# Four image layers on one core: where the constants of the scans are made, and where their first pixels are loaded

## The chip, the cores and the metric

One core of a Trainium2 chip runs the whole kernel. The metric is the device time in microseconds (us); the time of a kernel is the median of several executions. Times inside an execution come from the hardware profiler. It names the engines PE (matrix products), PEld (its weight loads), DVE (vector), ACT (scalar and table functions), POOL (GpSimd) and SP (which here only issues transfers; ACT issues some, too). PSUM is the memory that PE writes to, in eight banks; SBUF is the working memory; DRAM is the memory outside the engines.

## The reference

The input is x of shape (4, 64, 128, 128) in float32: four images of 64 channels. Four layers follow each other. The first is a gate in the spectrum with attention; the second mixes Fourier modes and routes to experts; both are left out here.

The third layer goes through a Hartley transform: it takes 20 x 20 modes of each channel, mixes the channels mode by mode, goes back to pixels, smooths along all four axes and keeps a band of columns:

```python
def _L2_conv_ref(x, w1):
    x_ht = dht_2d(x)
    out_ht = jnp.zeros((B, Cout, H, W), dtype=x.dtype)
    out_ht = out_ht.at[:, :, :M1, :M2].set(compl_mul2d(x_ht[:, :, :M1, :M2], w1))
    y = dht_2d(out_ht) / (H * W)
    y = gaussian_smoothing_4d(y)
    return y * mask
```

The fourth layer runs two selective scans (state of 16 per channel). The spectral one ("spe") takes each pixel as a sequence of 8 groups of 8 channels, the spatial one ("spa") all pixels of all images as one sequence. Each does:

```python
def mamba_fwd(x, in_w, conv_w, conv_b, xproj_w, dt_w, dt_b, A_log, D, out_w):
    xi, z = jnp.split(x @ in_w.T, 2, axis=-1)
    xc = jax.nn.silu(causal_conv4(xi) + conv_b)
    dt, Bm, Cm = jnp.split(xc @ xproj_w.T, [dt_rank, dt_rank + D_STATE], axis=-1)
    dt = jax.nn.softplus(dt @ dt_w.T + dt_b)
    # h = exp(dt * A) * h + dt * Bm * xc ;  y = h . Cm + D * xc
    return (y * jax.nn.silu(z)) @ out_w.T
```

Both results are normalized in groups, put through silu, weighted by a softmax of two numbers (`att_w`) and added to the layer's input.

## The kernel before

**The stages.** `layers_0_to_2` runs the first three layers. For each of the four images it does the gate, the attention, the mixing, the experts and `hartley`, which leaves 20 x 20 modes of the image in the tile `xht` (400 x 2 x 4 numbers on each of 128 partitions). Then `hartley_back` mixes and returns to pixels for all images together. `layer3` follows with the scans.

**`hartley_back`, the way back.** First come four groups of mode products: the weights `mw` arrive in halves, one from SP's queue and one from ACT's (L1192), behind the table `pack_g`; PE multiplies them by columns of `xht`. Then comes a loop over the image rows, four at a time. `over_p(h4)` makes a pair of banks (`ps_s`, 32 small products), which DVE and ACT copy to `dt` in turn (`move`). `over_q(h4)` makes for each half of the images (`bp`) four products into a bank (`ps_pt` or `ps_m`, of which there are two each). ACT copies its columns to `st`, with a margin of four columns for the scan that runs along rows (L1237); DVE copies them to `sk`, without the margin (L1238, L1239). After every eight rows, SP stores `st` into `x2s` in DRAM (L1242), and ACT's queue stores `sk` into `x2k` (L1243). `st` and `sk` exist three times. The loop calls `over_p` one step ahead of `over_q`.

**`layer3`, the scans.** It opens new pools, loads the table `pack_d` and calls `scan_constants`, which copies parts of the table to tiles of their own (`c_gm16w`, `c_gme`, `c_sel`, `c_spe_w0` and so on), makes two products of small weights on PE (into a bank of `ps_m`), takes exponentials on ACT, and scales the identity by the softmax of `att_w` (`by_0`, `by_1`, `by_x`). Then it allots the states `h`, the inputs `dB` (eight tiles each) and two tiles `A10` and `A11` for pixels of the spectral scan, clears parts of these on POOL, and calls `scans`.

The pixels of the spectral scan come in groups of four units. `spe_load(m, g)` loads one eighth of group `m` into `A1[m % 2]` by two transfers on SP of eight partitions each (L1373, L1374), so that a group takes 16 transfers; it reads `x2k`. Of a unit, `do_x` makes two sums of products and ACT makes `xc` and `zs` of them (L1400, L1401); `do_dt` makes `dt` in nine steps, in one of which the identity sums four tiles in a bank; `do_put` writes `dt` and `dtx` to DRAM and `do_copy` brings them back spread over partitions; then `do_exp`, `do_dB`, `do_scan` and `do_hc` work on eight parts, and `do_sums` and `do_y` close the unit.

**What sets the order.** Inside `scans` the order of PE, DVE, ACT and POOL is written out by hand: every step has a due time, and the steps are issued in the order of these times. SP's transfers are not part of that. Outside of it a scheduler orders the instructions of each engine by when it reckons that they can run. It also puts in the waits: for data, for a tile or bank that is used again, and for memory in which a tile of a closed pool lay. A queue executes in order, so an instruction that waits holds up those behind it.

Of the kernel before, what the change touches and what calls it, by code (L numbers as in the profile page):

```python
# [19 lines left out]
NM = 20  # L20
# [13 lines left out]
CPX = 64  # L34
ORDER = (0, 2, 4, 6, 1, 3, 5, 7)
# [276 lines left out]
class Net:  # L312
# [67 lines left out]
    def layers_0_to_2(self, x2s, x2k):  # L380
        tc, nc = self.tc, self.nc
        with ExitStack() as ctx:
            const = ctx.enter_context(tc.tile_pool(name="const", bufs=1))
            self.k = self.unpack(const, "a")
            self.eps = const.tile([128, 1], F32, name="eps")
            nc.vector.memset(self.eps, 1e-5)
            self.nmz = [const.tile([128, 4, 128], F32, name=f"nmz{i}") for i in range(2)]
            for t in self.nmz:
                nc.gpsimd.memset(t, 0.0)
            self.xht = const.tile([128, NM * NM, 2, NB], F32, name="xht")  # L390
            with tc.tile_pool(name="big", bufs=4) as big, tc.tile_pool(name="srw", bufs=1) as srw:
                self.big = big
                self.sr1 = srw.tile([128, 32, C], F32, name="sr1")
                nc.scalar.dma_start(self.sr1, self.d["sr1"])
                self.gate_constants(const)
                for b in range(NB):
                    with self.banks(f"a{b}", s=2, pt=2, m=2):
                        xf = self.spectral_gate(b)
                        kT, va, hold = self.keys_values(b, xf)
                    with self.banks(f"b{b}", sp=6, o=1, m=1):  # L400
                        xc = self.attention(b, xf, kT, va)
                    hold.close()
                    with self.banks(f"c{b}", s=2, pt=2, m=2):
                        self.fourier_mixing(b, xc)
                        self.experts(b, xc)
                        self.hartley(b, xc)
            with self.banks("d", s=2, pt=2, m=2):
                self.hartley_back(x2s, x2k)
# [770 lines left out]
    def hartley_back(self, x2s, x2k):  # L1179

        tc, nc = self.tc, self.nc
        with tc.tile_pool(name="hb", bufs=1) as hp:
# [26 lines left out]
            with tc.tile_pool(name="hs", bufs=3) as sp:  # L1209
                rows, dts = {}, {}  # L1210

# [34 lines left out]
                for h4 in range(0, N, 4):  # L1246
                    if h4 + 4 < N:
                        over_p(h4 + 4)
                    over_q(h4)

    def layer3(self, x2s, x2k, y1, ye):
        tc, nc = self.tc, self.nc
        self.x2s, self.x2k, self.y1, self.ye = x2s, x2k, y1, ye
        with ExitStack() as ctx:
            pool = lambda name, bufs: ctx.enter_context(tc.tile_pool(name=name, bufs=bufs))
            const = pool("c3", 1)
            self.psum = ctx.enter_context(tc.tile_pool(name="psum3", bufs=1, space=PSUM))
# [4 lines left out]
            with tc.tile_pool(name="d3", bufs=1) as dp:  # L1264
                self.scan_constants(const, self.unpack(dp, "d"))
# [4 lines left out]

            self.big2 = [const.tile([128, 10 * 4 * CPX + 96], F32, name=f"A1{i}") for i in range(2)]
            self.A1 = [t[:, : 10 * 4 * CPX].rearrange("p (t x) -> p t x", t=10) for t in self.big2]
            for A in self.A1:
                nc.gpsimd.memset(A[0:64, 0:3, :], 0.0)
                nc.gpsimd.memset(A[64:128, 0:2, :], 0.0)
# [3 lines left out]
            self.dBs = [const.tile([128, 2, 512], F32, name=f"dB{q}") for q in range(8)]  # L1279
# [13 lines left out]
    def scan_constants(self, pool, k):  # L1293
        nc = self.nc
        self.c3 = c3 = {}

        def keep(name, shape):
            c3[name] = pool.tile(list(shape), F32, name="c_" + name)
# [317 lines left out]
    def scans(self, us):  # L1616
# [7 lines left out]
        for ci, u in enumerate(us):  # L1624
# [4 lines left out]
            else:  # L1629
# [4 lines left out]
                for g in range(8 if i == 0 else 0):  # L1634

                    do(-48.0 + 3 * g if m > 1 else -48.0, self.spe_load, m, g)
# [133 lines left out]
    def run(self):  # L1770
        with self.tc.tile_pool(name="dram", bufs=1, space=DRAM) as dp:
# [4 lines left out]
            self.layers_0_to_2(x2s, x2k)  # L1776
            self.layer3(x2s, x2k, y1, ye)
# [21 lines left out]
```

## Time and profile before

| what | value |
|---|---|
| median of 3 runs | 7353.47 us (7347.41 to 7354.81) |
| the profiled execution | 7342.41 us |
| its span, first to last instruction | 7340.7 us |
| mean granted clock of PE | 0.953 |
| busy PE, DVE, ACT, POOL | 90%, 74%, 65%, 49% of the span |
| way back, loop over rows, about | 3440 to 3564.5 us |
| first product of the scans | 3581.65 us |

Times in views are counted from the span's start. The shares of busy time are averages over stages with different limits: POOL does almost nothing in the first half and is busy all the time in the second. A row of the chain of waits has a start, a length and the engine or transfer on which the end of the span depended there. A row of the waits has who waited, for whom, the sum in us, how often, and the longest.

### The profile page before, as it was taken

The numbers are of one execution on the slowest core, as the hardware profiler recorded it, in microseconds if no ns is written. First come the engines' busy times: TensorE is split into PE (matmuls) and PEld (weight loads), VectorE is DVE, ScalarE is ACT, GpSimd is POOL, SyncE is SP. The second block draws the span as 40 slices with busy tenths as digits, with TensorE's granted clock in tenths as the row PEclk, the third lists the DMA queues.
The fourth block names the chain that finished last, engine by engine and source line by source line (L and its number), as shares of the span: only waits on it lengthen the run. The fifth ranks groups of instructions, "written<-read, shape, count | busy, mean of one in ns | idle before, by whom it ended". The sixth has DMA issues, their size and how long they took to land.

```text
span 7340.7 us, 106844 instructions
## 1 busy us (share of the span) xinstructions
PE 6632.5 (90%) x39058; PEld 2873.7 (39%) x39058; DVE 5408.6 (74%) x7737; ACT 4771.6 (65%) x7768; POOL 3607.2 (49%) x1908
## 2 busy tenths in 40 slices
PE   8998999989999899988899999999899888888897
PEld 6335553347335553346422223222322332332333
DVE  3665546563565546663599999999999899899896
ACT  2564636553564536652588888888788787887885
POOL 1000000000000000000399999999999899899896
PEclk9998989989999989987899999999999999999998
DMA  3000010002000110002455555555454464564554
GB/s 90 1 1 1 28 47 1 1 1 74 1 1 1 28 47 1 1 1 106 133 145 150 149 147 150 149 149 148 133 149 146 129 183 142 143 172 137 156 162 119
DMA packets 364110, 647.03 MB, mean 88 GB/s; under 512 B 46784, under 2 KB 219584, under 8 KB 362048
## 3 DMA queue, kind: packets, MB, share of 16 engines
q1 hardware_dynamic: 357680, 609.91, 30.0%
q10 hardware_dynamic: 5904, 30.28, 1.2%
q8 instruction: 308, 5.05, 0.3%
q14 instruction: 218, 1.79, 0.1%
HBM read 517.80 MB, written 122.22 MB: 87 GB/s over the span
## 4 chain that ended last, share of the span: by engine, by line
PE 48%; DVE 19%; issue 10%; POOL 10%; ACT 8%; DMA 4%; SPq 1%; POOLq 0%; DVEq 0%; ACTq 0%
PE ps_sp L330 14%; DVE h L1493 9%; PE ps_s L330 8%; PE ps_m L330 7%; POOL hc L1520 6%; PE ps_o L330 6%; PE ps_pt L330 4%; DVE dB L1488 3%; POOL dB L1488 2%; PE ps_dx L330 2%; PE ps_y L330 2%; DMA s_dx<-ddx 2%; ACT dA L1472 2%; DVE big L1061 2%; PE ps_m L811 1%
## 5 line engine op out<-in xcount | busy, mean ns | idle before, releaser
L1520 POOL TENSOR_TENSOR hc<-h,C 128x966 f32<-128x966 f32 (+3 forms) x1128 | 2437.4, 2240 | 118.7 <-DVE h L1493 93.2
L1493 DVE TENSOR_TENSOR_SCAN h<-dA,h,dB 128x483 f32<-128x483 f32 (+1 forms) x1200 | 1348.4, 1166 | 54.5 <-ACT dA L1472 54.5
L755 DVE TENSOR_REDUCE nmz<-ps_sp 128x1 f32<-128x320 f32 x2048 | 895.8, 485 | 622.5 <-PE ps_sp L330 613.2
L771 ACT ACTIVATE big<-ps_sp 128x512 f32<-128x512 f32 (+1 forms) x1536 | 830.6, 592 | 720.3 <-PE ps_sp L330 719.0
L1493 DVE TENSOR_TENSOR_SCAN h<-dA,dB 128x512 f32<-128x512 f32 (+2 forms) x1072 | 1222.0, 1190 | 4.0 <-ACT dA L1472 3.9
L930 POOL TENSOR_TENSOR aw<-pack_a 128x128 f32<-128x128 f32 x8 | 3.5, 456 | 2189.8 <-PE ps_m L330 2189.8
L1488 POOL TENSOR_TENSOR dB<-s_dx,B 128x1024 f32<-128x1024 f32 (+5 forms) x450 | 993.7, 2210 | 15.4 <-DMA s_dx<-ddx 6.7
L330 PE MATMUL ps_sp<-uT,kT 32*128 32x512 f32 x3072 | 924.2, 649 | 1.4 <-ACT big L771 0.8
L330 PE MATMUL ps_dx<-dtx,c_sel 128*128 128x483 f32 (+3 forms) x1420 | 754.5, 613 | 188.0 <-DVE dB L1488 186.5
L1488 DVE TENSOR_TENSOR dB<-ps_dx,B 128x1024 f32<-128x1024 f32 (+5 forms) x750 | 810.9, 1083 | 147.4 <-PE ps_dx L330 146.5
L1472 ACT ACTIVATE dA<-s_dt,c_spa_a 128x483 f32<-128x483 f32 (+3 forms) x1232 | 760.8, 640 | 179.0 <-DVE h L1493 176.9
L330 PE MATMUL ps_sp<-kT,qT 32*128 32x320 f32 x4096 | 817.3, 499 | 3.9 <-ACT qT L736 3.3
L1472 ACT ACTIVATE dA<-s_dt,c_spe_a 128x448 f32<-128x448 f32 x1040 | 635.7, 632 | 155.0 <-DVE h L1493 154.2
L330 PE MATMUL ps_y<-hc,c_sum 128*32 128x483 f32 (+3 forms) x4512 | 680.1, 560 | 60.9 <-POOL hc L1520 54.3
L330 PEld LDWEIGHTS ps_dx<-dtx,c_sel 128*128 128x128 f32 x1420 | 225.8, 190 | 661.9 <-DVE dB L1488 225.4
L330 PEld LDWEIGHTS ps_sp<-uT,kT 32*128 32x128 f32 x3072 | 278.8, 185 | 438.3 <-issue 243.0
L330 PE MATMUL ps_o<-big,va 128*32 128x512 f32 (+1 forms) x3072 | 415.6, 613 | 0.0
L330 PE MATMUL ps_s<-pack_a,big 128*64 128x128 f32 (+4 forms) x2832 | 371.0, 307 | 45.6 <-DMA big<-in_x 19.6
L330 PEld LDWEIGHTS ps_sp<-kT,qT 32*128 32x128 f32 x4096 | 358.2, 190 | 57.2 <-issue 36.6
L330 PEld LDWEIGHTS ps_s<-pack_a,big 128*128 128x128 f32 (+2 forms) x2832 | 329.1, 180 | 67.5 <-issue 25.7
L330 PEld LDWEIGHTS ps_y<-hc,c_sum 128*32 128x32 f32 x4512 | 124.9, 109 | 509.4 <-issue 306.8
L454 POOL MEMSET big<- 64x128 f32 x4 | 0.8, 200 | 627.5 <-PE ps_s L330 420.0
(391 smaller groups left out, 10376.4 us busy)
## 6 DMA issues: line engine op xcount, KB each, us to landing
s_dt<-ddt SPq DMA_DIRECT2D x520, 256.0 KB
s_dt<-ddt SPq DMA_DIRECT2D x544, 241.5 KB
s_dx<-ddx SPq DMA_DIRECT2D x195, 256.0 KB
s_dx<-ddx SPq DMA_DIRECT2D x204, 241.5 KB
ddt<-dt SPq DMA_DIRECT2D x65, 256.0 KB
ddx<-dtx SPq DMA_DIRECT2D x65, 256.0 KB
A<-x2s SPq DMA_DIRECT2D x136, 121.2 KB
ddt<-dt SPq DMA_DIRECT2D x68, 241.5 KB
```

The source lines that it names most:

```text
L330: self.nc.tensor.matmul(out, lhsT, rhs, start=start, stop=stop)
L454: nc.gpsimd.memset(mag[64:128, 32, :], 0.0)
L755: nc.vector.tensor_reduce(self.nmz[n % 2][:, j, at : at + 1], p[:, :KEYS], AX.X, ALU.max, negate=True)
L771: nc.scalar.activation(slot(m, 2 * wu + q)[rows], p[rows], AF.Exp)
L811: nc.tensor.transpose(p[:, 128 * j : 128 * j + 128], o[:, 128 * j : 128 * j + 128], k("ident"))
L930: nc.gpsimd.tensor_tensor(aw[i], k(f"aw{i + 1}"), k("sg"), ALU.mult)
L1061: nc.vector.scalar_tensor_tensor(acc(i), y, gate[:, p : p + 1], acc(i), ALU.mult, ALU.add)
L1472: self.nc.scalar.activation(t(u["dA", q][sg][:, u["lo"] : u["n"]]), t(u["dt", q]), AF.Exp, scale=a)
L1488: eng.tensor_tensor(v(dB[:, :, x:y]), v(d), v(u["BC"][0][:, :, x:y]), ALU.mult)
L1493: self.nc.vector.tensor_tensor_scan(h[:, lo:n], u["dA", q][sg][:, lo:n], self.dBs[q][:, sg, lo:n], init, ALU.mult, ALU.add)
L1520: self.nc.gpsimd.tensor_tensor(v(hc), v(self.hs[q][:, :, at]), v(u["BC"][1][:, :, at]), ALU.mult)
```

## The change

`layer3` now opens its pool of constants first and calls `hartley_back` inside it. `hartley_back` loads `pack_d` at the start of its loop over rows, calls `scan_constants` behind the rows of `h4 == 8`, and calls `spe_load(0, g)` for all eight `g` behind those of `h4 == 80`; `scans` leaves the first group's loads out. The two lines in the loop are placed in the program's order; the scheduler may still move what they issue.

To have the memory for that at the same time, three kinds of tiles get new places. `xht` and the convolution weights `sr1` of the first layer move to a pool (`held`) that lives to the end. `A10`, the identity and the three scaled identities lie in the old `xht`, which is free after the mode products; `dB0` and `dB1` lie in the old `sr1`. The clearing of `A10` and `A11` moves into `scan_constants`.

```diff
-    def layers_0_to_2(self, x2s, x2k):
+    def layers_0_to_2(self):
...
-            self.xht = const.tile([128, NM * NM, 2, NB], F32, name="xht")
-            with tc.tile_pool(name="big", bufs=4) as big, tc.tile_pool(name="srw", bufs=1) as srw:
+            self.sr1 = self.held.tile([128, 32, C], F32, name="sr1")
+            with tc.tile_pool(name="big", bufs=4) as big:
                 self.big = big
-                self.sr1 = srw.tile([128, 32, C], F32, name="sr1")
...
-            with self.banks("d", s=2, pt=2, m=2):
-                self.hartley_back(x2s, x2k)
...
-    def hartley_back(self, x2s, x2k):
+    def hartley_back(self, x2s, x2k, const):
...
-            with tc.tile_pool(name="hs", bufs=3) as sp:
+            with tc.tile_pool(name="hs", bufs=3) as sp, tc.tile_pool(name="d3", bufs=1) as dp:
                 rows, dts = {}, {}
+                kd = self.unpack(dp, "d")
...
                     over_q(h4)
+                    if h4 == 8:
+                        self.scan_constants(const, kd)
+                    if h4 == 80:
+                        for g in range(2 * NB):
+                            self.spe_load(0, g)
...
             const = pool("c3", 1)
+            with self.banks("d", s=2, pt=2, m=2):
+                self.hartley_back(x2s, x2k, const)
...
-            with tc.tile_pool(name="d3", bufs=1) as dp:
-                self.scan_constants(const, self.unpack(dp, "d"))
...
-            self.big2 = [const.tile([128, 10 * 4 * CPX + 96], F32, name=f"A1{i}") for i in range(2)]
-            self.A1 = [t[:, : 10 * 4 * CPX].rearrange("p (t x) -> p t x", t=10) for t in self.big2]
-            for A in self.A1:
-                nc.gpsimd.memset(A[0:64, 0:3, :], 0.0)
-                nc.gpsimd.memset(A[64:128, 0:2, :], 0.0)
...
-            self.dBs = [const.tile([128, 2, 512], F32, name=f"dB{q}") for q in range(8)]
+            spare = self.held.tile([128, 32, C], F32, name="sr1").rearrange("p (i s a) c -> p i s (a c)", i=2, s=2)
+            self.dBs = [const.tile([128, 2, 512], F32, name=f"dB{q}") if q > 1 else spare[:, q] for q in range(8)]
...
     def scan_constants(self, pool, k):
         nc = self.nc
         self.c3 = c3 = {}
+        self.old_xht = self.held.tile([128, NM * NM, 2, NB], F32, name="xht").rearrange("p m s b -> p (m s b)")
+        self.big2 = [self.old_xht[:, :A1_SIZE], pool.tile([128, A1_SIZE], F32, name="A11")]
+        self.A1 = [t[:, : 10 * 4 * CPX].rearrange("p (t x) -> p t x", t=10) for t in self.big2]
+        for A in self.A1:
+            nc.gpsimd.memset(A[0:64, 0:3, :], 0.0)
+            nc.gpsimd.memset(A[64:128, 0:2, :], 0.0)
+        rest = [self.old_xht[:, A1_SIZE + 128 * i : A1_SIZE + 128 * i + 128] for i in range(4)]
...
         def keep(name, shape):
-            c3[name] = pool.tile(list(shape), F32, name="c_" + name)
+            if name in ("id", "by_0", "by_1", "by_x"):
+                c3[name] = rest.pop()
+            else:
+                c3[name] = pool.tile(list(shape), F32, name="c_" + name)
             return c3[name]
...
-                    do(-48.0 + 3 * g if m > 1 else -48.0, self.spe_load, m, g)
+                    if m:
+                        do(-48.0 + 3 * g if m > 1 else -48.0, self.spe_load, m, g)
...
-            self.layers_0_to_2(x2s, x2k)
-            self.layer3(x2s, x2k, y1, ye)
+            with self.tc.tile_pool(name="keep", bufs=1) as self.held:
+                self.xht = self.held.tile([128, NM * NM, 2, NB], F32, name="xht")
+                self.layers_0_to_2()
+                self.layer3(x2s, x2k, y1, ye)
```

More of the change, by code (lines that the diff above doesn't have):

```diff
@@ L34 @@
 CPX = 64
+A1_SIZE = 10 * 4 * CPX + 96
 ORDER = (0, 2, 4, 6, 1, 3, 5, 7)
```

## The prediction

> **What bounds the kernel now.** I first read the busy time by stage, with stages cut where the work changes: the way back of the Fourier layer (3440 to 3564.5 us), the gap behind it, the ramp of the scans, and the scans. The columns are length, busy time (instructions) of PE, PEld, DVE, ACT and POOL, granted clock, DMA share, GB/s.
>
> ```profile
> core 0: us, PE busy (x) PEld busy (x) DVE busy (x) ACT busy (x) POOL busy (x), PEclk, DMA share, GB/s
> 3440.00:3564.50 124.50, 123.53 (x1524) 89.98 (x1515) 51.14 (x144) 40.95 (x80) 0.00 (x0) 0.99 0.41 154
> 3564.50:3581.60 17.10, 0.68 (x4) 0.52 (x4) 10.20 (x51) 1.81 (x4) 2.75 (x4) 0.62 0.57 120
> 3581.60:3621.00 39.40, 28.48 (x48) 10.60 (x48) 3.64 (x4) 22.73 (x30) 7.84 (x5) 0.73 0.42 99
> 3621.00:7340.00 3719.00, 3282.52 (x12028) 1127.67 (x12026) 3451.70 (x3582) 2984.69 (x4729) 3519.33 (x1797) 0.97 0.53 148
> ```
>
> The way back is PE's: 123.5 of 124.5 us, with DVE at 41% and ACT at 33%. The scans are POOL's and DVE's (95% and 93%), and the change gives them nothing to save. Between the two lie 17.1 us in which PE does 0.68 us. That is all that a move of this kind can win, and some. The waits say who is waited for, and the chain of waits says in which order:
>
> ```profile
> PE ps_m L330 <- DMA A<-x2k: 16.4, 1, 16.4
> ```
>
> ```profile
> 3564.28 0.21 DVE sk L1239
> 3564.51 2.81 DMA x2k<-sk
> 3567.64 0.33 SPq L1373
> ...
> 3570.41 5.66 DMA A<-x2k
> 3576.09 5.50 DMA A<-x2k
> 3581.59 0.06 issue
> 3581.65 3.77 PE ps_m L330 x4
> 3585.47 1.28 ACT L1400
> 3586.76 1.17 ACT xc L1400
> ```
>
> The last store of x2k must land (3567.6) because the tiles of the scans lie where its source lay. Then SP issues 16 loads of the first pixels, some 0.7 us apart, and the first product of the scans waits for the sixteenth. The constants are not in this chain. The timeline shows them beside it, from 3567.62 to 3576.29:
>
> ```profile
> 3567.60 1.28 ACT L1315 ACT_TABLE_LOAD   x1 [3.65 <-DMA x2k<-sk]
> ...
> 3567.76 1.05 DVE L1302 COPY c_gme<-pack_d 128x512 f32<-128x512 f32 x1
> ...
> 3571.65 0.41 DVE L1310 COPY c_spa_bc<-pack_d 128x512 f32<-128x512 f32 x1
> ...
> 3576.01 0.28 DVE L1332 TENSOR_SCALAR c_by_x<-pack_d,c_att_m 128x128 f32<-128x128 f32 x1
> ```
>
> **Part 1, the gap.** In the built order of the changed kernel, the 16 loads of the first pixels stand on SP among the stores of x2s, the last of them ahead of the store of rows 80 to 87; the 16 loads of the second pixels, into memory that is now free as early, are spread in the same way, and three of them remain behind the last store. So nothing of the first load is left in the gap. What is late next? PE needs its banks: the last copy out of them ends at 3564.49, so PE starts at 3564.6 instead of 3581.65. It is now at full clock, and its four passes take 1.88 us (as the next unit's, at 3603.5) instead of 3.77, so they end at 3566.5. That is not yet the gain: ACT's first result still goes to memory that the last stores of x2s and x2k are read from, and its table load holds that wait in the built order. They landed at 3567.6; I add 0.2 us for the loads that run beside them. Table load 1.28, so xc starts at 3567.8 + 1.3 = 3569.1, against 3586.76: **17.7 us earlier**. From xc on the chain is ACT's eight steps and PE's sums, with the same instructions in the same order, none of them waiting for what was moved. The puts and copies of dt and dtx move along. The six passes at 3593.6 ran at half clock; whether they do so again depends on where idle time falls: 2 us either way.
>
> **Part 2, the constants inside the way back.** 45 instructions on DVE, 3 on ACT and 2 PE products (four passes, 0.68 us) now stand among the rows 4 to 16 of a loop that PE fills. DVE has the room on average (2.3 us idle of each 3.85), but the order has them in blocks. By the rows of before, DVE ends the first bank of rows 4 at 3450.27; then the first 21 copies follow at one go, then the second bank of rows 4, then ten more, then the two banks of rows 8. PE is released twice by these copies, since both products borrow a bank of the two that the loop's own results need: the first product (nominal 3453.99) needs the second bank of rows 4, the second product that of rows 8.
> The price of the block is the question. As traced, its 21 copies and products took from 3567.62 to 3571.98, 4.36 us, but with POOL's four memsets beside them: c_gme took 1.05 us and c_spa_bc, of the same shape, 0.41. The Trainium skill (SBUF — State Buffer, "Who interferes with whom") says that VectorE in its two-port modes and GpSimd take turns on one pair of ports, each for a whole instruction. By it the moved block, with POOL's memsets done long before, takes what its undisturbed rows give: 2.8 us (each step at its start-to-start time, 0.13 for 128x128, 0.35 for 128x512, 0.07 for a column).
> - At 2.8 us: the second bank of rows 4 is free at 3453.5, no stall at the first product. The ten others (1.6 us, with the wait for that product) and the two banks of rows 8 end at 3456.2; the second product would be due at 3454.7: stall 1.5 us. With the 0.7 us of the products PE is **2.2 us late**, and, PE being full, stays so.
> - At 4.36 us: stalls of 1.2 and 2.0 us, plus 0.7: 3.9 us late.
> I take 2.3 us, since nothing of POOL is near; ends 0.7 (all stalls absorbed) and 4.6. ACT's table load (1.28) and three exponentials there fit into its 2.5 us idle stretches, and its store of x2k waits for a DVE copy that is late by 2.8 us, which the block itself covers.
>
> **Part 3, the loads on SP and the DMA engines.** The period of eight rows is 7.69 us. SP gains two loads in most of them (six in a row once, 4.2 us): 0.7 us apart by the rows of before, and here and there a wait of 3.35 us for a store of x2k to land (issued 3564.2, landed 3567.55), beside two stores (0.65 us). That is up to 5.4 of 7.69 us; the stores that stand behind them have three buffers. The DMA engines are at 0.41 of this stage, and all 32 loads held 0.57 of them for some 22 us, 12.5 of the 73 us that are free. Cost 0; if the cover went, see the second rival.
>
> **Part 4, what the new memory layout moves.** Loads of mw and pack_g start the mode products:
>
> ```profile
> q1 hardware_dynamic: 338, 4.05, 59.6%
> q10 hardware_dynamic: 332, 2.30, 32.6%
> ```
>
> These are packets, MB and share of SP's and ACT's queue from 3355 to 3372 us. PE waits 14.05 us for the first tile of mw, of which SP's half stands behind pack_g (2.69 + 0.98 MB). In the changed order ACT's four loads, the first of which started at 3355.33, come after its copy to xht, at 3358.4. For 3 us SP then has the engines alone. At the traced share of ACT (2.30 of 6.35 MB) that frees 0.45 MB of about 0.42 MB a us: 1.1 us earlier. The Trainium skill (DMA: Bandwidth & Descriptors, "Queues, rings and completion order") says that an engine takes packets from its queues in turn; by equal turns the estimate would be 1.5 us. I take **1.1**, ends 0 and 2.
> The old tiles that now hold A10, the identity, by_* and dB0 and dB1 cost 0: in the built order the scans' instructions wait for the same engines as before.
>
> **Sum.** -17.7 + 2.3 - 1.1 = -16.5 us. The profiled execution took 7342.41 us (span 7340.7), so 7325.9 in its own terms. The median of the three runs is 7353.47, 11 us above it; the stages concerned run once, so I subtract the same: **7337.0 us**. The runs shown are 7.4 us apart, so 0.2% (14.7 us) is about what a measurement of this kernel can tell from no change, and the forecast is just beyond it.
>
> **Rivals.**
> - *The block costs what it was seen to cost, and the clock is less kind.* 4.6 us in part 2, no gain in part 4, and the passes behind xc slower by 2 us: -17.7 + 4.6 + 2 = -11.1, 7342.4 us. Also what a moderately late SP would leave. For it: c_gme's 1.05 us, and PE at half clock after 3 us of idle (from 3357.5 to 3360.3). Against it: POOL is idle there, and no single stall comes near 3 us.
> - *SP becomes the bound of the way back (slower than before).* If each of two loads in a period waited for a full landing of 3.4 us beside the store's 3.35 and 0.65 of issues, the period on SP would be 10.8 instead of 7.69 us. Over 16 periods that is 50 us, less 15.4 that three buffers forgive: 34 late, net +18, 7371 us. It decides from 7.69 us in a period. For it: loads here used about half of the engines and kept 0.7 us each. Against it: in the gap ten loads ran in 7 us without waiting for one another's landing.
> - *It doesn't do what it says*: excluded by the order, as far as the first load goes.
>
> **How the numbers follow.** Forecast and its better variants 0.62; the first rival, with a draw of the medians the wrong way, 0.27; SP's bound 0.08 and the unforeseen in the scans (1% of 3719 us would do) 0.03. The range goes from 7329 (all of part 1, 2 us of part 4, 0.7 of part 2, warm passes, and a few us of scatter) to 7347 (the first rival and 4 us of scatter).
>
> **What would show it.** Right: the first product of the scans starts within 1 us of the last copy of sk; xc 4.5 us behind that; PE in the way back stalls for 1 to 2 us once near rows 8 to 16; mode products start about 1 us earlier relative to the copy of xht. Wrong: PE waiting for a load of A at the start of the scans, SP's stores of x2s falling behind ACT's copies, or a stage of the scans that is not 3756 to 3760 us from the first product to the end (3759 now).

## The result, and the profile after

The changed kernel takes 7331.42 us, median of 11 runs (7325.84 to 7341.55), against 7353.47 us for the kernel before, also of 11 runs (7339.41 to 7356.52). The ratio is 0.9974, with a 95% interval from 0.9966 to 0.9982. The profiled execution took 7329.77 us (span 7327.9, mean granted clock 0.955), 12.6 us less than the profiled execution of before.

The busy time by stage of the changed kernel, with the same columns as the table of before, cut at the last copy of `sk` (3566.8) and at the first product of the scans (3567.0):

```profile
core 0: us, PE busy (x) PEld busy (x) DVE busy (x) ACT busy (x) POOL busy (x), PEclk, DMA share, GB/s
3441.00:3566.80 125.80, 124.85 (x1523) 90.59 (x1515) 57.13 (x189) 42.54 (x84) 0.00 (x0) 0.99 0.47 166
3566.80:3567.00 0.20, 0.00 (x0) 0.02 (x1) 0.02 (x2) 0.00 (x0) 0.00 (x0) 1.00 1.00 362
3567.00:3605.70 38.70, 26.68 (x48) 9.82 (x48) 5.60 (x8) 22.78 (x30) 7.80 (x5) 0.82 0.36 107
3605.70:7327.00 3721.30, 3283.45 (x12028) 1126.61 (x12026) 3451.42 (x3582) 2985.48 (x4729) 3520.90 (x1797) 0.97 0.54 148
```

The gap of 17.1 us is 0.2 us long. The 45 DVE instructions of the constants have moved from the gap into the way back (144 instructions there before, 189 now), where PE is as full as it was. The granted clock of the ramp is 0.82 instead of 0.73. PE's first four passes, behind 1.2 us of idle instead of 16.4, take 1.96 us instead of 3.75; the two of `c_spe_wdt`, a little later, now stand behind 3.5 us of idle instead of 1.5, and take 2.07 us instead of 1.16.

The chain of waits from the end of the way back to `xc` (start, length, engine or transfer):

```profile
3566.31 0.30 DVE sk L1237
3566.61 0.21 DVE sk L1238
3566.81 0.02 issue
3566.83 4.06 DMA x2k<-sk
3570.89 0.02 issue
3570.91 0.04 ACTq L1412
3570.95 0.03 issue
3570.98 1.28 ACT L1412
3572.26 0.01 issue
3572.27 1.18 ACT xc L1412
```

The loads of the first pixels are gone from it. What is left between the last `sk` and `xc` is the landing of the last stores, 4.2 us, and the table load.

The constants in the timeline of the changed kernel, between rows 4 and 16:

```profile
3451.27 0.42 DVE L1314 COPY c_gme<-pack_d 128x512 f32<-128x512 f32 x1
...
3453.60 0.41 DVE L1322 COPY c_spa_bc<-pack_d 128x512 f32<-128x512 f32 x1
...
3454.94 0.48 PE L331 MATMUL ps_m<-pack_d 4*128 4x128 f32 x2
...
3455.46 0.29 DVE L1325 COPY c_spa_wdt<-ps_m 128x128 f32<-128x128 f32 x1 [0.17 <-PE ps_m L331]
...
3455.92 0.48 PE L331 MATMUL ps_m<-pack_d 8*128 8x128 f32 x2
```

`c_gme` takes 0.42 us instead of 1.05, and the whole block of 21 goes from 3451.14 to 3453.93, 2.8 us.

Absolute times don't compare well between executions. Over the fourteen profiles of this study the `xm` copy of the last image, ahead of which all kernels run the same instructions (e9b issues one transfer more), starts between 3354.1 and 3367.3 us, and the stretch from the first `dB` on DVE to the end is 3722.5 to 3728.8 us long. So the stages are compared by their lengths. The table has them for all kernels, from the starts in the timelines ("mode" is the first product of `mw`, "dt" the first copy of `dt`, "sk" the end of the last copy of `sk`, "dB" the first `dB` on DVE):

| kernel | xm to mode | mode to dt | dt to sk | sk to xc | xc to dB | sum | ratio to before (95%) |
|---|---|---|---|---|---|---|---|
| before | 16.29 | 71.12 | 121.78 | 22.28 | 29.63 | 261.10 | |
| before_again | 16.95 | 71.28 | 121.78 | 22.85 | 29.38 | 262.24 | 0.9993 (0.9981 to 1.0004) |
| changed | 15.37 | 71.46 | 123.29 | 5.47 | 28.83 | 244.42 | 0.9974 (0.9966 to 0.9982) |
| after_again | 15.71 | 71.25 | 123.15 | 5.65 | 28.44 | 244.20 | 0.9980 (0.9971 to 0.9989) |
| e1_const_only | 15.61 | 71.46 | 123.62 | 20.18 | 28.71 | 259.58 | 0.9996 (0.9988 to 1.0004) |
| e2_loads_only | 15.94 | 71.38 | 121.78 | 18.77 | 29.81 | 257.68 | 0.9993 (0.9985 to 1.0001) |
| e3_loads_in_scans | 16.02 | 71.45 | 123.93 | 5.63 | 29.20 | 246.23 | 0.9976 (0.9966 to 0.9985) |
| e4_xc_memory | 15.20 | 71.45 | 124.24 | 3.54 | 28.45 | 242.88 | 0.9974 (0.9963 to 0.9985) |
| e5_second_loads | 15.11 | 71.46 | 125.62 | 5.50 | 29.78 | 247.47 | 0.9982 (0.9973 to 0.9990) |
| e6_pack_g_behind | 9.21 | 72.25 | 124.17 | 5.67 | 29.35 | 240.65 | 0.9967 (0.9955 to 0.9979) |
| e7_loads_twice | 15.24 | 71.46 | 122.73 | 5.76 | 28.87 | 244.06 | 0.9973 (0.9962 to 0.9985) |
| e8_pool_beside | 15.77 | 71.46 | 126.38 | 5.66 | 29.29 | 248.56 | 0.9976 (0.9966 to 0.9986) |
| e9b_const_in_gap | 16.17 | 71.45 | 122.52 | 9.32 | 29.79 | 249.25 | 0.9981 (0.9972 to 0.9990) |
| e11_table_early | 9.13 | 72.25 | 123.58 | 2.20 | 28.95 | 236.11 | 0.9965 (0.9953 to 0.9978) |

### The profile page after: what moved, and what is told of

Same layout as the page of the kernel before. It is cut to its first block, busy times and chain, and to the rows that moved or that the text cites. A ratio compares the mean times of both kernels' runs of the same rounds, so it can differ in the third digit from the quotient of the medians.

```text
span 7327.9 us, 106846 instructions
## 1 busy us (share of the span) xinstructions
PE 6630.8 (90%) x39058; PEld 2869.5 (39%) x39058; DVE 5405.7 (74%) x7737; ACT 4772.8 (65%) x7768; POOL 3608.7 (49%) x1908
## 4 chain that ended last, share of the span: by engine, by line
PE 49%; DVE 18%; issue 9%; POOL 9%; ACT 9%; DMA 4%; SPq 1%; POOLq 0%; DVEq 0%; ACTq 0%
PE ps_sp L331 14%; PE ps_m L331 9%; DVE h L1505 9%; PE ps_s L331 7%; PE ps_o L331 6%; POOL hc L1532 6%; PE ps_pt L331 4%; DVE dB L1500 3%; PE ps_y L331 3%; PE ps_dx L331 3%; DVE big L1059 2%; ACT dA L1484 2%; DMA s_dx<-ddx 2%; DMA big<-in_sr 1%; PE ps_m L809 1%
## 5 line engine op out<-in xcount | busy, mean ns | idle before, releaser
L1505 DVE TENSOR_TENSOR_SCAN h<-dA,h,dB 128x483 f32<-128x483 f32 (+2 forms) x900 | 1025.2, 1167 | 52.9 <-ACT dA L1484 52.9
L1505 DVE TENSOR_TENSOR_SCAN h<-dA,dB 128x512 f32<-128x512 f32 (+2 forms) x804 | 929.7, 1188 | 4.0 <-ACT dA L1484 4.0
L1500 POOL TENSOR_TENSOR dB<-s_dx,B 128x952 f32<-128x952 f32 (+6 forms) x300 | 672.6, 2244 | 14.6 <-DMA s_dx<-ddx 7.9
L1500 DVE TENSOR_TENSOR dB<-ps_dx,B 128x952 f32<-128x952 f32 (+4 forms) x600 | 646.0, 1079 | 14.5 <-PE ps_dx L331 13.7
L1505 DVE TENSOR_TENSOR_SCAN h<-dA,h,sr 128x483 f32<-128x483 f32 (+2 forms) x300 | 342.6, 1162 | 0.0
L1500 POOL TENSOR_TENSOR sr<-s_dx,B 128x952 f32<-128x952 f32 (+2 forms) x150 | 336.6, 2246 | 0.3
```

What stands on the lines that cost most here:

```text
L1500: eng.tensor_tensor(v(dB[:, :, x:y]), v(d), v(u["BC"][0][:, :, x:y]), ALU.mult)
L1505: self.nc.vector.tensor_tensor_scan(h[:, lo:n], u["dA", q][sg][:, lo:n], self.dBs[q][:, sg, lo:n], init, ALU.mult, ALU.add)
```

## The experiments

**How far one profile can be trusted: both kernels a second time.**

> The kernel before once more, for a second profile of it. Theory (the stretch from the xm copy to the first dB is steady, and the last stores of before land 3.1 us after the last sk copy): 261.1 us and 3.1 us within 0.5 us, so that the 16.7 us between the two kernels in this stretch and the 1.1 us of later landing are the change's. Rival (the landing scatters by 1 us between executions): the stores land 4 us or more after the last sk copy, and the stretch is 262 us or more, so that the changed kernel's later landing is no cost of the change.

Before again: the stores land 3.12 us after the last `sk` copy in both profiles (read at the start of the table load that waits for them), and the sum is 262.24 instead of 261.10, 1.1 us longer, which lies in the start of the mode products (0.7) and in the loads of the gap (0.6). So the landing supports the theory, and the stretch varies a little more than the theory allowed. The medians of this one program on one chip are 7344.80 and 7348.19 us.

> The changed kernel once more, as the measure for the scatter between executions. Theory (the stretch from the first dB to the end scatters by 2 us either way between executions, and the stages before the xm copy by 6 us or more): the distances from xm to the last sk copy and from there to xc come out within 1 us of the first profile of the changed kernel (210.1 and 5.5 us), and the time within 3 us of 7331.4. Rival (the 12.8 us between the two first profiles and the 22.1 us between the medians are both real and the sum missed something): the median lies 20 us or more under before again, and the stretch from xm to the first dB is shorter by more than 15 us.

The changed kernel again: 210.1 us from `xm` to the last `sk` and 5.65 to `xc`, as the theory said; the median is 7335.56 us, 4.1 above the first, a little outside of the 3 us. In the mean of two profiles each, the stretch is 261.67 us before and 244.31 after: the change gains 17.4 us there. The two ratios come to 19 and 15 us of 7350. The rival, that the 22 us between the first two medians are all the change's, falls.

**e1: constants early, loads in the gap.** On the changed kernel:

```diff
-                    if h4 == 80:
+                    if h4 == N - 4:
+                        nc.vector.tensor_copy(self.A1[0][:, 9, 0:1], rows[1][1][:, 7, 0:1])
                         for g in range(2 * NB):
                             self.spe_load(0, g)
```

> The constants stay in the way back, as in the changed kernel; the 16 loads of the first pixels are put back behind the last row group (a copy of one column of the last sk into A10 makes them wait for it). Theory (the gap was the loads, not the constants): the first product starts about 17 us after the last sk copy and xc about 22 us after it, as before the change (17.2 and 22.3), so the time is that of the kernel before, +1.4 for the constants in the way back and -0.9 for the earlier mw loads: within 2 us of before, 16 to 18 us over the changed kernel. Rival (the constants made in the gap were a share of it, the loads hid only a part): xc comes 4 us or more sooner than 22 us after the last sk copy, and the time lies that much under the kernel before.

The ratio is 0.9996: nothing is left of the gain. The chain of waits of e1 runs through the loads as that of before does:

```profile
3565.87 3.99 DMA x2k<-sk
3569.86 0.02 issue
3569.88 5.01 DMA xht<-x2k
3574.88 0.02 issue
3574.90 5.44 DMA xht<-x2k
3580.34 0.56 issue
3580.90 3.76 PE ps_m L331 x4
```

`xc` starts 20.2 us after the last `sk`, 2.4 us sooner than in the two profiles of before (22.3 and 22.9). The first seven loads start from 3565.93 on, before the stores have landed, since their memory is not that of `st` and `sk` any more. The rival asked for 4 us or more. The sum of the stretch is 2.1 us under the mean of before, and the time can't be told from it. Moving the constants alone is worth no more than that.

**e2: loads early, constants and `pack_d` behind the way back.**

```diff
-            with tc.tile_pool(name="hs", bufs=3) as sp, tc.tile_pool(name="d3", bufs=1) as dp:
+            with tc.tile_pool(name="hs", bufs=3) as sp:
...
-                    if h4 == 8:
-                        self.scan_constants(const, kd)
...
+            with tc.tile_pool(name="d3", bufs=1) as dp:
+                self.scan_constants(const, self.unpack(dp, "d"))
             self.const, self.small = const, pool("st", 2)
```

> The loads of the first pixels stay at h4 == 80; the load of pack_d and the constants go behind the way back, as before the change. Theory: pack_d is 2.42 MB, some 7 us at 350 GB/s behind its issue and the stores beside it, and the VectorE block of 2.8 us stands behind it, so that the first product starts 11 to 13 us after the last sk copy instead of 0.2, with the clock at half; the way back is 1.4 us shorter without the constants; in all 6 to 12 us over the changed kernel, and 5 to 12 us under before. Rival (the constants are hidden behind the stores' landing, which xc waits for anyway): xc starts no more than 6 us after the last sk copy, and the time is that of the changed kernel or 1.4 us less.

The ratio is 0.9993, and the sum of the stretch 4.0 us under the mean of before, against the 5 to 12 expected. But this is not what moving the loads alone is worth, and in one point the text above is wrong: before the change `pack_d` was issued at 3438.9, ahead of the way back, and only its use stood in the gap; here its load is in the gap too. What the loads alone are worth is read from e9b. The chain of waits of e2:

```profile
3565.20 10.05 DMA pack_d<-in_pack_d
3575.25 0.14 issue
3575.38 1.19 PE ps_m L331 x4
3576.57 2.36 issue
3578.93 3.77 PE ps_m L331 x4
```

`pack_d` needs 10 us beside the last stores, not 7, and 3.7 us of products and copies follow until `c_spe_w` is there. With the first product 13.65 us behind the last `sk`, the sum is 13.4 us above the changed kernel's, against 6 to 12 expected. The way back, without constants in it, takes 121.78 us to the hundredth as before; so the constants' cost there is 1.4 to 1.5 us (123.29 and 123.15). That is known to some 0.7 us: the other variants that make the same constants there have 122.7 to 124.2 (leaving out e5 and e8, which hold the loop up in other ways), and e9b, without them, has 122.5.

**e9b: only the constants in the gap.** `pack_d` lies at the other end of the memory, lands early, and the constants have memory that no store holds (two of their copies already run ahead of the last `sk`):

```diff
+            d3 = tc.tile_pool(name="d3", bufs=1, side="right")
+            self.d3 = d3.__enter__()
             with self.banks("d", s=2, pt=2, m=2):
                 self.hartley_back(x2s, x2k, const)
...
+            self.scan_constants(pool("c4", 1), self.kd)
+            d3.__exit__(None, None, None)
```

> The loads stay at h4 == 80 and pack_d lands early (in memory at the far end, issued ahead of pack_g); only the constants themselves are made behind the way back, in memory that shares nothing with st and sk, so that they need not wait for the stores. Theory (each of the two chains that the change took out of the gap fills most of it by itself, and e2's 13.7 us were pack_d's landing, 10 us, and 3.7 us of block): here the block alone stands between, so that the first product starts about 3 to 5 us after the last sk copy, xc 6 to 10 us after it instead of 5.5, and the time is 1 us less to 4 us more than the changed kernel's. Rival (the constants themselves, not their load, make e2 slow): the first product again starts 10 us or more after the last sk copy, 8 us or more over the changed kernel.

The first product starts 3.10 us after the last `sk` and `xc` 9.3 us after it, both in the theory's range. The sum is 4.9 us above the changed kernel's mean, just over the 4 us expected; the two medians (7333.48 here) are too near for the time to show it. Against before, the sum is 12.4 us shorter, and the ratio, 0.9981, is clear of 1: with the constants still in the gap, the early loads keep most of the gain. That is in the new layout; in the old one the constants waited for the last stores, too, and how much the loads alone would keep there was not run. What holds `xc` in e9b's timeline is not the product:

```profile
3580.15 3.75 PE L331 MATMUL ps_m<-xht,c_spe_w 128*128 128x512 f32 x4 [2.27 <-DVE c_spe_w L1325]
...
3584.66 0.28 DVE L1349 TENSOR_SCALAR xht<-pack_d,c_att_m 128x128 f32<-128x128 f32 x1
3585.08 1.28 ACT L1417 ACT_TABLE_LOAD   x1 [2.69 <-DVE xht L1349]
3586.37 1.18 ACT L1417 ACTIVATE xc<-ps_m,c_spe_cb 128x512 f32<-128x512 f32 x1
```

PE is at half clock again after its idle stretches (0.50 granted, 3.75 us for four passes), and the table load comes behind the last of the constants. So two chains stood side by side in the gap, if each is asked for alone: the loads (`xc` at 20.2 us, e1) and the block of constants (9.3, e9b). Taking the first away uncovers the second. The third, the landing of `pack_d` with the block behind it (18.8), was put there by e2 and stands in neither kernel.

**e3: the place in the program.**

```diff
-                    if h4 == 80:
-                        for g in range(2 * NB):
-                            self.spe_load(0, g)
...
-                    if m:
-                        do(-48.0 + 3 * g if m > 1 else -48.0, self.spe_load, m, g)
+                    do(-48.0 + 3 * g if m > 1 else -48.0, self.spe_load, m, g)
```

> Of the changed kernel only the place of the first pixels' loads in the program is undone: they stand in the scans again, the memory that they fill (the old xht) stays as the change made it. Theory (the memory lets the loads go early, the place in the program does not matter, since the queue is filled in order of readiness): the loads are issued among the stores as in the changed kernel, the first product starts within 0.5 us of the last sk copy, and the time is the changed kernel's within 2 us. Rival (the place decides): the loads stand behind the last stores, xc comes 22 us after the last sk copy, 16 us over the changed kernel.

The first product starts 0.21 us after the last `sk`, and the time is the changed kernel's (0.9976). It is the memory that lets the loads go early; where they stand in the program changes nothing.

**e7: the loads twice.**

```diff
                         for g in range(2 * NB):
                             self.spe_load(0, g)
+                            self.spe_load(0, g)
```

> The changed kernel with each of the 16 first loads issued twice (the same bytes to the same place), which adds 16 issues of about 0.55 us to the SP queue of the way back. Theory (SP has room in each row group of 7.69 us): the last sk copy comes at the same distance from the first row group within 1 us, and the time is the changed kernel's within 2 us. Rival (SP is the bound of the way back once the loads stand in it): 16 more issues lengthen the way back by up to 9 us, and the changed kernel itself paid about as much for its own 16.

122.73 us from the first `dt` to the last `sk`, not longer than the 123.15 and 123.29 of the changed kernel, and the same time (0.9973). SP has room for twice the loads; the second rival of the prediction falls. What gave way are the loads of the second pixels: most of them now start behind the last `sk`, the last one 7.8 us after it, and the stage times show no cost of that.

**e5: the second pixels' loads ahead of the last stores.**

```diff
+                    if h4 == 88:
+                        for g in range(2 * NB):
+                            self.spe_load(1, g)
...
-                    if m:
-                        do(-48.0 + 3 * g if m > 1 else -48.0, self.spe_load, m, g)
+                    if m > 1:
+                        do(-48.0 + 3 * g, self.spe_load, m, g)
```

> The changed kernel with the loads of the second pixels placed at h4 == 88, so that none of them stands in the SP queue behind or between the last stores. Theory (three loads issued with the last stores delay their landing): the table load of silu starts 3.1 us after the last sk copy, as the stores landed before the change, instead of 4.2; the time falls by 1 us. Rival (the landing of the last stores is as late without them): 4.2 us again, no change.

4.21 us again, without a single load behind the last stores, so the gain did not come. The bytes moved, in 40 slices of the six us from 3562.5 in the kernel before, of the seven us from 3564.8 in the changed kernel, and of the seven us from 3564.35 in e5:

```profile
GB/s 28 28 0 0 0 0 0 0 0 206 397 383 339 412 328 361 430 416 348 380 397 353 412 324 364 430 402 347 278 14 0 0 0 0 0 0 0 0 0 0
```

```profile
GB/s 24 24 24 0 0 0 0 0 303 379 366 416 318 380 416 392 331 404 404 303 287 220 325 419 308 274 202 154 165 193 182 111 53 29 18 0 0 0 0 0
```

```profile
GB/s 415 380 357 155 24 36 48 94 315 379 328 379 340 381 380 382 385 404 402 402 400 380 406 382 109 25 24 24 24 24 0 0 0 0 0 0 0 0 0 0
```

The stores of before end all together. In the changed kernel the last us, loads included, runs at about half of the full rate; in e5 there is a tail of 0.9 us at 24 GB/s, about one sixteenth, as if one of the 16 engines were behind. The landing signals in the traces say the same. A store has sixteen of them, a load of eight partitions eight. Those of the last store of `sk`, in us after the last copy:

| kernel | moved beside the last stores | signals of the last store |
|---|---|---|
| before, before_again | nothing | 16 from 2.65 to 2.84 |
| changed, after_again | three loads of pixels | 8 from 2.82 to 2.98, 8 from 3.55 to 4.26 |
| e2 | `pack_d` and three loads | 16 from 5.98 to 7.00 |
| e5 | one packet of instructions | 15 from 2.60 to 2.80, one at 3.83 |

All other variants have loads there, and look like the changed kernel: eight signals from 2.66 to 2.99, eight from 3.31 to 4.28. So the loads do hold up half of the landing, and the theory's mechanism holds; the rival, that the stores are as late without them, does not. What e5 gained on fifteen signals it lost on one: in each of its four last stores one signal comes 1.0 us behind the others. The packet of instructions took 0.8% of 16 engines' seven us, 0.9 us of one engine (from the view of transfers in that stretch):

```profile
q8 instruction: 1, 0.02, 0.8%
```

That it is what the late signal waited for is inferred from the two lengths, since the trace doesn't name the engine of a signal.

e5 also costs something: its way back is 2.4 us longer than in the mean of the changed kernel's two profiles. The rows of the waits in it, of SP and of PE:

```profile
SPq L1388 <- DMA x2k<-sk: 14.2, 6, 6.2
```

```profile
PE ps_pt L331 <- ACT st L1236: 2.1, 1, 2.1
```

Loads put close behind the stores that they read wait for these on SP, up to 6.2 us, with the stores of `x2s` queued behind them; then `st` is late, and so is PE. This is the mechanism of the second rival, set off by placing the loads badly. Such a wait alone does not make the cost: e7 has some of up to 6.0 us, and PE waits 0.2 us there.

**e8: POOL at work beside the constants.**

```diff
+        nc.gpsimd.tensor_copy(self.big2[1][:, :64], dt[:, :64])
+        for _ in range(3):
+            nc.gpsimd.memset(self.big2[1], 0.0)
         for key in ("gm16w", "gme", "goh", ...
```

> The changed kernel with three clears of the whole of A11 (128 x 2656) on GpSimd beside the constants, started by a copy of 64 columns of the last dt. Theory (VectorE and GpSimd share a port, so that copies that took 1.05 us beside GpSimd's clears in the gap took 0.42 us alone): the copies that stand beside the clears take 1 us instead of 0.42 (512 columns) and the block of 21 takes 4 us or more instead of 2.8. Rival (the copies of before were longer for another reason, the DMAs or the memory they lay in): 0.42 and 2.8 us again.

POOL starts at 3453.17, when the block of 21 is already done in 2.8 us; the clears meet the copies that follow (timeline of e8):

```profile
3453.17 7.31 POOL L1315 MEMSET A<- 128x2656 f32 x3
...
3453.66 2.00 DVE L1325 COPY c_spe_z<-pack_d 128x128 f32<-128x128 f32 x1
...
3455.61 2.62 DVE L1325 COPY c_spe_bc<-pack_d 128x512 f32<-128x512 f32 x1
```

`c_spe_z` took 0.22 us in the changed kernel and 2.00 here, `c_spe_bc` 0.42 and 2.62. A clear takes 2.44 us, and a copy waits out the clear that it meets. The way back grows by 3.2 us, to 126.38. So the theory holds for the mechanism, and what it says of before, that its copies were long because of POOL's four short clears, fits. Transfers are not the reason: in e9b `c_gme` ran beside the last stores without clears and took 0.42 us.

**e4: memory of their own for `xc` and `zs`.**

```diff
+            self.xz = pool("xz", 3)
             with self.banks("d", s=2, pt=2, m=2):
                 self.hartley_back(x2s, x2k, const)
...
-        u["xc"], u["zs"] = self.tile2("xc", u, 3), self.tile2("zs", u, 3)
+        u["xc"], u["zs"] = (self.xz.tile([128, 512], F32, name=key)[:, u["lo"] : n] for key in ("xc", "zs"))
```

> The changed kernel with memory of their own for xc and zs, in a pool opened before the way back, so that they share nothing with st, sk and dt. Theory (in the changed kernel xc, started 5.5 us after the last sk copy, waits for the last stores to land, because its tile lies where st and sk were): the table load for silu no longer waits for a DMA and stands beside the first products, xc starts about 2.5 us after the last sk copy, when the products end, and the time falls by about 3 us (2 to 3.4). Rival (it is the loads or something else that holds xc, or what follows xc waits for the stores all the same): xc or its followers start as in the changed kernel, and the time stays within 1 us.

The table load no longer waits for a transfer, and `xc` starts 3.54 us after the last `sk`, 1.9 to 2.1 us earlier (timeline of e4):

```profile
3576.27 1.28 ACT L1413 ACT_TABLE_LOAD   x1 [2.77 <-PE ps_m L331]
3577.56 1.17 ACT L1413 ACTIVATE xc<-ps_m,c_spe_cb 128x512 f32<-128x512 f32 x1
```

It is 1 us short of the theory, as the table load now holds `xc`'s wait for the products instead of standing beside them. The time (0.9974) can't tell 2 us.

**e6: `pack_g` behind the first weights.**

```diff
+                    if t == 0:
+                        kg = self.unpack(hp, "g", self.xht[:, NM * NM - 1, 1, NB - 1 :])
...
+        if behind is not None:
+            self.nc.vector.tensor_copy(t[:, :1], behind)
         self.nc.sync.dma_start(t, self.d[name])
```

> The changed kernel with the load of pack_g (2.69 MB) issued behind the first two halves of mw (a copy of one column of xht into it makes it wait), so that the first mode's weights have the DMA engines first. Theory (the mode products' start is set by bytes ahead of the first mw tile in the DMA engines, which is why the earlier mw loads gained 0.9 us): the products start 5 to 7 us sooner after the xm copy than the 15.4 us of the changed kernel, and the time falls by 4 to 7 us. Rival (the stage is bound by all its bytes, so that the later mw tiles or gbc are late instead): the products start sooner, but the last of them end as before, and the time stays within 1 us.

The timeline of e6:

```profile
3368.96 0.33 SPq L1189 DMA_DIRECT2D mw<-in_mw  x1
...
3370.01 0.33 SPq L346 DMA_DIRECT2D pack_g<-in_pack_g  x1
...
3375.86 12.93 PE L331 MATMUL ps_s<-xht,mw 128*64 128x8 f32 x120 [6.97 <-DMA mw<-in_mw]
```

The mode products start 9.2 us after `xm` instead of 15.4 to 15.7, and the stage behind them is 0.9 us longer: 5.4 us gained, and 0.9967. So the start of the stage is a matter of the bytes ahead of the first tile.

**e11: the three gains together, the table load first.** On e4 and e6 together:

```diff
+                    if h4 == N - 4:
+                        warm = const.tile([128, 1], F32, name="warm")
+                        nc.scalar.activation(warm, rows[1][0][:, 7, :1], AF.Silu)
```

> Three edits on the changed kernel: memory of their own for xc and zs (as in e4), the load of pack_g behind the first mw halves (as in e6), and a silu of one column of the last st into a tile that nothing reads, so that ScalarE loads its table right behind the last st copy, beside the first products. Theory (the gains stand in a row on one chain): 5.4 us from the earlier mode products, 1.9 us from xc that waits for no store, 1.3 us from the table load beside the products, so xc starts 2.2 us after the last sk copy, and the time is 8 to 9 us under the changed kernel's, some 7323 us. Rival (what is gained before the scans is given back in them, or the table load pushes the last x2k stores back and these hold the next step): the stage times fall as said, but the time stays within 3 us of the changed kernel's.

`xc` starts 2.20 us after the last `sk`, as said, and the median is 7323.21 us (0.9965): the best of all, 8 us under the first median of the changed kernel and 12 under the second. Its interval overlaps that of the changed kernel, so the stage times carry the claim: 236.11 against 244.31 us. One part of the rival is there too. In the chain of waits of e11 the wait for the last stores has moved one step on, to the table load of `sp_hi`:

```profile
3572.01 0.21 DVE sk L1241
3572.22 0.02 issue
3572.24 4.13 DMA x2k<-sk
3576.37 0.02 issue
3576.39 0.04 ACTq L1432
3576.43 0.13 issue
3576.56 1.28 ACT L1421
3577.84 0.01 issue
3577.86 0.69 ACT sp_hi L1432
```

`sp_hi` starts 5.65 us after the last `sk`, 3.2 us earlier than in the changed kernel (3575.68 against 3566.80, 8.9 us) and about as much as `xc` (3.3). The 4.13 us of landing are now the longest piece there.

## Why the prediction was right, point by point

The forecast was 7337.0 us, a gain of 16.5; the median came out at 7331.4, a gain of 22.1. By stages, as the mean of two profiles each, the gain is 17.4.

- *What bounds the kernel.* Right: the gap was all that could be won, way back and scans gave nothing, and the loads were the longer chain in it. What the prediction did not ask is what each half of the change is worth. Of the 17.4 us, the early loads alone, in the new layout, keep 12.4 (e9b) and the early constants alone 2.1 (e1); the last 5 us need both. Both were moved in one change, so its sum did not need that point.
- *Part 1, -17.7.* From the last `sk` to `xc` -17.0: 22.57 before in the mean, 5.56 now. The step that was mis-sized is "I add 0.2 us for the loads that run beside them": the stores land 4.2 and 4.35 us after the last `sk`, where they landed after 3.12 us in both profiles of before, so the term is 1.1 to 1.2 us. The landing signals show the loads to be the cause (e5); e4 shows that this landing does hold `xc`. The clock, "2 us either way", came out at -0.9 from `xc` to `dB`, which is not clear of the scatter: the variants with `xc` as early have 28.4 to 29.8 there.
- *Part 2, +2.3.* +1.4 (123.22 against 121.78), within the ends 0.7 and 4.6. The choice between the two prices of the block was right: 2.8 us, as the rule of the Trainium skill (SBUF — State Buffer, "Who interferes with whom") had it, not the 4.36 us of the traced block. e8 shows the rule at work. The mis-sized term is the stall, put at 1.5 us beside 0.7 for the products: the products took 0.96 (the two rows above), so that 0.5 us are left for stalls. The one stall of 1 to 2 us that was to show it is not there: the waits of PE have no row in those rows of the loop.
- *Part 3, 0.* Right, and with room to spare (e7). The second rival needed 10.8 us in a period; only e5, with loads right behind the stores that they read, shows its mechanism, at 2.4 us. One reading against that rival was wrong: the loads in the gap did wait for one another's landing. In the chain that the prediction shows, the load of 3576.09 starts as that of 3570.41, the eighth before it, lands; the first eight start 0.35 us apart, and only the later ones 0.7. It did no harm, as e7 shows.
- *Part 4, -1.1.* -1.1 (16.62 before, 15.54 now, in the mean of two). The wait itself is one row of the waits of the changed kernel:

```profile
PE ps_s L331 <- DMA mw<-in_mw: 13.1, 1, 13.1
```

It was 14.05 us before. Equal turns of the queues would have given 1.5. The runs don't decide between the two: the two profiles of before differ by 0.7 us in this stage, so that the agreement to a tenth is luck. That the stage hangs on the bytes ahead of its first tile, e6 shows.
- *Sum.* -17.0 - 0.9 + 1.4 - 1.1 is -17.5 before rounding, and the 0.2 us that the stage from mode to `dt` is longer make it -17.4; the prediction's -16.5 is within 1 us, in part by luck: its terms missed by 0.7 us (part 1), 0.9 (the clock) and 0.9 (part 2), not all the same way. The other 5 us of the first pair of medians are not the change's as far as shown: medians of the same program differ by 3 us (before_again) and 4 us (after_again), and the first profiles alone would give 12.8 us of span.

Most of the prediction's signs were there, too: the first product 0.2 us after the last `sk`, and `xc` 5.3 us behind that instead of 4.5. The mode products start 0.9 us sooner by the first pair of profiles. From the first product to the end it is 3760.9 us in the first profile, 0.9 above the 3756 to 3760 foretold, and 3759.6 in the second; before again has 3760.0.

## What to carry to other kernels

A gap between two stages can be several chains side by side. The profile names the one that ends last, and taking that one away gains only what it is longer than the next (here 12.4 of 17.4 us), so list what else starts at the gap's beginning and ask of each when it would end by itself. An experiment that takes one half of a change back can put something new into the gap, as e2 did with `pack_d`: look at what it moved before believing its time. What keeps work from starting early can be the memory of a closed pool and not the place in the program: find the first instruction that waits for a transfer only because of where its tile lies. And for a gain of 0.2%, compare lengths of stages between two marks in the profile, not absolute times or single spans.

## What the runs showed of the hardware that was not expected

- The last stores (two of 276 KB and two of 260 KB) landed 3.12 us after the last copy in both profiles of before, and 4.0 to 4.5 us after it where loads of eight partitions were issued beside them. Only half of the last store's sixteen landing signals were late (e5); beside `pack_d` all were, by 3.3 us or more (e2).
- One signal of sixteen, 1.0 us late, is enough to hold a store as long as three loads do (e5: 4.21 us). The packet of instructions that fits it is of 16 KB, and took 0.95 us.
- A VectorE copy that meets a GpSimd clear of 2.44 us takes up to 2.62 us instead of 0.42 (e8).
- SP had eight loads in flight in the gap of before: from the ninth on, each started when the load eight before it had landed (the first 2.6 us after its issue, the ninth 5.7).
- The first four passes of the scans took 3.77 us behind 11.1 and 2.4 us of idle with 1.2 us of small products between (e2), and 3.75 us behind only 1.2 and 2.3 us of idle with 0.7 us of products between (e9b); behind 1.2 us of idle alone they took 1.96 us (the changed kernel).
- The `xm` copy came up to 13 us apart over the profiles, with the same instructions ahead of it; two profiles of one program differ there by 1.4 us (before) and 2.6 (the changed kernel). What makes the rest is open.
